# Copies of the late experts' outputs made on TensorE in place of DRAM, last writes split 48 and 16, and a new drawn order, in a two-layer MetaFormer kernel

## The chip, the core and the metric

The kernel runs as one program on one core of a Trainium2 chip. The core has five engines that run their own instruction streams in order: TensorE (PE, matrix products), VectorE (DVE), ScalarE (ACT), GpSimd (POOL) and SyncE (SP). SP, ACT and POOL also issue transfers between DRAM and the on-chip memory, which 16 DMA engines carry out. The metric is the device time of one execution in microseconds; lower is better. The time before is a median of 3786.38 us over three runs (3786.0 to 3797.89).

## What is computed

The input x has 32 images of 56 x 56 positions and 128 channels, all float32. Two layers run one after the other, each with a token mixer and a feed-forward part, both with a residual:

```python
# layer 0
x = x + conv_binary_3x3(batchnorm_sign(layernorm(x)))       # signs of weights and inputs
t = t + moe(layernorm(t))           # 8 experts of 128x128, the best 2 for each token
# layer 1
x = x + gate * (layernorm(triangle_product(a, b)) @ Wz + bz) # over each image's 56x56 grid
t = t + expert_choice(layernorm(t))
```

The change lies around the last step. Of an image's 3136 tokens, each of 64 experts chooses the 8 with the highest softmax probability (over the tokens):

```python
logits = einsum('bsd,ed->bse', x, gate_w); probs = softmax(logits, axis=1)
vals, idx = top_k(probs.transpose(0, 2, 1), 8)               # per image and expert: 8 tokens
pooled = einsum('bked,bke->bed', gathered, topv)             # the 8 tokens, summed by weight
h = gelu(pooled @ weight1 + bias1); out = h @ weight2 + bias2 # 64 experts, 128 -> 512 -> 128
outputs[b, idx] += topv * out        # ONE output row goes to eight tokens, with eight weights
```

So one output row of an expert for an image is written eight times, each time with another factor, added to eight different tokens. A token can be chosen by several experts.

## The kernel before

**Tiling.** The 32 images are worked as 16 pairs, p = 0 to 15. A pair's 6272 tokens are 7 units of 128 x 7 tokens, 128 channels each. A first pass over all 112 units gathers the batch statistics of layer 0 (until about 600 us). Then the pairs follow at a period of about 190 us, several of them overlapped: the convolution of one pair runs beside the mixture of experts, the triangle product and the last gates of earlier ones.

**The stages of a pair that matter here.** `moe_experts` (L812 on) loads, for each of 49 tiles of 128 tokens, the gates of 8 experts, repeated over all partitions, into a tile gb (SP, L821), multiplies it by the transposed tokens xT (VectorE, L827), and PE sums eight matmuls into acc (L832). xT is copied out of the transposes trm by ACT (L583). Before that the routing runs through PE's ps_rl and ps_r, a chain of small VectorE operations, and the transpose trg (L797) of the gates. `tri_turn` makes the transposes trt; `gate_turn` stores the pair's result to `out`; `top8` finds the 8 tokens of each expert and gathers them (POOL, L1222); `pool_rows` sums them and ends in the transpose tr_p.

**The late experts.** The 64 experts' weights (32 MB) are streamed twice. `late_experts(False, g)`, 16 groups g of four experts, serves the 26 images of pairs 0 to 12 and runs between the stages of pairs 13 to 15. `late_experts(True, g)` serves the last three pairs (LAST) at the end. Both load the weights (L1412, L1414), form ph (L1479), the transposes trh, the gelu on ACT, po (L1525), and add the bias on VectorE (L1533) into `side2.ap[:, 5, :]`, 128 rows: 4 experts x 32 images.

For pairs 0 to 12 the images form two lots of 14 and 12 (LOTS). Before, the group's rows are written to DRAM (`o_d`, L1541), then read back for each lot and expert with each row repeated eight times (L1551), into a tile `eo` with 112 or 96 rows for four experts. `eo` shares the buffers tagged xT. VectorE multiplies it by the gains (L1558), and POOL adds each expert's rows to the tokens in `out` by an indirect transfer (L1575), in which a lot's next addition waits for the last one's landing:

```python
for j in range(NE):
    nc.sync.dma_start(
        eo.ap[:rows, j, :],
        o_d[g][j, i0:i1, :].unsqueeze(1).to_broadcast([i1 - i0, K1, C]),
    )
```

A one-element memset, `between` (L1316), stands between POOL operations of different lots.

**The last three pairs.** `last_sums(p)` reads the chosen tokens of each of these pairs (POOL, L1666, 8 times 128 rows) into rows_last and builds a matrix m that says which experts' outputs belong to which row, so that each row is written once with all its additions. `last_load(half)` reads the outputs of 32 experts back from `o_last_d` into at_last (SP, L1689); `last_out_rows(p, half)` multiplies m by them (PE, L1708), adds them to the rows (VectorE, L1720) and writes four times 128 rows (POOL, L1731), so 12 writes for each half of the experts.

**What sets the order.** Each operation is recorded by `op(engine, ns, r=, w=, land=)` with what it reads and writes, a cost, and for transfers a time `land`. The stages get a rank from the table TICK. `Order.run` then plays the program through by these costs, picks for each engine the ready operation of lowest rank, subject to a fixed number of buffers for each tag (gb 5, xT 4, ps 8 PSUM banks, x 15, u 6), and emits the instructions in the order so found. The order of each engine is thus fixed when the program is built; on the chip each engine runs its own list and waits where something is late. SP's list holds all loads and most stores, so a transfer that waits for its buffer holds all that stand behind it.

Of the kernel before, what the change touches and what calls it, by code (L numbers as in the profile page):

```python
# [12 lines left out]
F32 = mybir.dt.float32  # L13
# [14 lines left out]
C = 128  # L28
N7 = 7
# [9 lines left out]
    "fetch": (1.58, 3.45, 5.52, -1.97, 9.89, 8.41, 11.94),  # L39
    "sign": (-0.24, 0.69, 0.62, 6.29, 6.36, 10.44, 7.52),  # L40
    "conv": (1.26, 2.47, 6.82, 8.46, 10.49, 11.27, 13.74),
    "conv_back": (3.04, 3.74, 6.89, 9.11, 10.54, 11.48, 14.87),
    "moe_turn": (4.55, 4.08, 9.93, 10.17, 12.05, 12.07, 15.21),
    "moe_gates": (7.93, 6.46, 10.3, 10.32, 15.22, 13.8, 15.72),
    "moe_experts": (10.11, 8.23, 10.44, 10.38, 15.35, 13.82, 17.26),
    "moe_add0": (14.4, 13.58, 10.89, 13, 17.91, 16.49, 17.47),
    "moe_add1": (12.35, 12.05, 11.31, 12.55, 16.09, 14.74, 18.98),
    "tri_turn": (16.03, 16.94, 19.18, 18.34, 19.2, 18.97, 19.62),
    "moe_stats": (4.06, 9.6, 11.95, 15.11),
    "moe_route": (6.11, 10.25, 12.5, 15.67),  # L50
    "tri_stats": (14.43, 14.07, 18.68, 19.34),
    "tri_b": (20.52, 21.37),
    "tri_a": (22.17, 21.41),
    "tri_z": (22.19,),
    "tri_out": (23.45, 23.11, 25.14, 25.06, 25.81, 28.13, 29.03),
    "gate_stats": (23.81, 25.31, 26.89, 30.24),
    "gate_turn": (25.22, 25.8, 26.84, 28.27, 29.66, 32.16, 31.08),
    "gate_logits": (26.8, 27.15, 28.55, 30.19, 30.4, 34.44, 34.71, 34.72),
    "clear": (32.94,),
    "top8": (36.55,),  # L60
    "pool_rows": (39.18,),
    "late_first": (27.19, 27.47, 30.26, 33.5, 37.45, 38.24, 40.16, 41.35, 43.38, 44.86, 45.85,
        48.06, 49.55, 51.3, 58.28, 60.22),
    "late_alone": (47.43, 50.82, 50.84, 53.47, 61.88, 67.39, 57.81, 65.6, 63.21, 71.67, 75.8,
        82.21, 97.17, 84.67, 68.82, 79.34),
    "last_sums": (70.63, 74.49, 77.96),
    "last_load": (68.66, 101.21),
    "last_rows": (91.82, 76.74, 99.71, 103.42, 119.45, 116.33),
# [4 lines left out]
NX, NY = 15, 6  # L73
# [212 lines left out]
def kernel(ctx: ExitStack, tc: tile.TileContext, a: dict, out: bass.AP):  # L286
# [12 lines left out]
    HB = B // 2  # L299
# [23 lines left out]
    make_identity(nc, ident)  # L323

# [42 lines left out]
    NL = 3  # L367
    LAST = range(NP - NL, NP)
    HB = 2 * ((NP - NL + 1) // 2)
    LOTS = ((0, HB), (HB, B - 2 * NL)) + tuple((2 * p, 2 * p + 2) for p in LAST)  # L370
# [3 lines left out]
    EH = E1 // 2  # L374
# [4 lines left out]
    o_d = [dram.tile([NE, B, C], F32, name=f"o_{g}") for g in range(E1 // NE)]  # L379
# [25 lines left out]
    with ExitStack() as c2:  # L405
# [21 lines left out]
        for t in lines:  # L427
# [3 lines left out]
            "x": NX, "u": NY, "ps": 8, "gb": 5, "xT": 4, "yl": 3,  # L431
            "st": 3, "q": 3, "lg": 1, "k1": 1, "k2": 1, "mk": 2, "d": 2,
            "gg": 2, "gT": 2, "rm": 4, "zq": 1, "lgT": 1,
            "m8": 2, "i8": 2, "sq": 2, "pg": 4, "near": 2, "pacc": 1, "ptc": NL + 1,
# [155 lines left out]
        def fetch(p, u):  # L590
            g = p * NU + u
            x_ = live[p]["x", u] = new("x", [128, N7, C], f"x_{NUT + g}")

            @op("SP", 360, w=parts(x_), land=1200)
            def _():
                nc.sync.dma_start(x_.ap, x_units[g])

        def sign(p, u):
# [3 lines left out]
            @op("SP", 360, r=[("y1_d", g)], w=[y], land=1200)  # L602
            def _():
                nc.sync.dma_start(y.ap, y1_d[g])
# [205 lines left out]
        def moe_experts(p, u, n):  # L810
# [8 lines left out]
            @op("SP", 360, r=[("gd", p, u)], w=[gb], land=1300)  # L819
# [136 lines left out]
        def tri_z(p):  # L956
# [71 lines left out]
            @op("SP", 360, r=[(zT, 0), (zT, 4)], w=[("z_d", p)], land=300)  # L1028
# [12 lines left out]
            for rg in range(4):  # L1041
                @op("SP", 720, r=[("z_d", p), zv], w=[(zv, rg)], land=300)
# [86 lines left out]
        def gate_turn(p, u):  # L1129
# [6 lines left out]
            @op(*issue, r=parts(x_), w=[("out", p, u)], land=1200)  # L1136
# [7 lines left out]
            @op(*issue, r=parts(y), w=[("y3", p, u)], land=1200)  # L1144
# [1009 lines left out]
```

## Time and profile before

| What | us |
|---|---|
| median of three runs | 3786.38 |
| the three runs | 3786.0, 3786.38, 3797.89 |
| the profiled execution, its own time | 3805.24 |
| its span, first to last instruction | 3803.4 |
| PE busy with matmuls in the span | 3427.8 |
| VectorE busy | 3191.5 |
| ScalarE busy | 2350.5 |
| POOL busy | 443.8 |
| mean granted clock of TensorE | 0.96 |

A profile line names an engine (PE, PEld for its weight loads, DVE, ACT, POOL, SP), a line of the code, an operation, and the tiles it writes and reads, with buffer numbers left out. "x128" is a count. After the bar stand the busy time in us, the mean of one in ns, and the idle time of the engine just before these instructions with what ended most of it. An engine's q (SPq) is its queue of transfers. In the list of waits a line says which instruction waited for which, for how many us in total, how often, and the longest. The chain of waits is followed back from the last instruction: at each step to what released it, or to the instruction before it on its engine. The rows of stages give, for a stretch of time, the busy time and count of each engine, the granted clock of TensorE (1.00 is full), the busy share of the DMA engines and GB/s. The profiled execution took 18.9 us more than the median of the runs.

### The profile page before, as it was taken

The numbers are of one execution on the slowest core, as the hardware profiler recorded it, in microseconds if no ns is written. First come the engines' busy times: TensorE is split into PE (matmuls) and PEld (weight loads), VectorE is DVE, ScalarE is ACT, GpSimd is POOL, SyncE is SP. The second block draws the span as 40 slices with busy tenths as digits, with TensorE's granted clock in tenths as the row PEclk, the third lists the DMA queues.
The fourth block names the chain that finished last, engine by engine and source line by source line (L and its number), as shares of the span: only waits on it lengthen the run. The fifth ranks groups of instructions, "written<-read, shape, count | busy, mean of one in ns | idle before, by whom it ended". The sixth has DMA issues, their size and how long they took to land.

```text
span 3803.4 us, 79485 instructions
## 1 busy us (share of the span) xinstructions
PE 3427.8 (90%) x28051; PEld 2791.8 (73%) x28051; DVE 3191.5 (84%) x10626; ACT 2350.5 (62%) x5438; POOL 443.8 (12%) x506
## 2 busy tenths in 40 slices
PE   7998999999999999999999999999999997876644
PEld 7886878787877777777777777777777775664422
DVE  7997979898989898989898989898989886765551
ACT  6997357575757666666666666666666664453420
POOL 0000000101010101010101010101010104234454
PEclk9999999999999999999999999999999998898667
DMA  7996747474747474747474747474747477687685
GB/s 292 358 356 226 256 155 268 151 272 148 276 150 268 146 268 153 269 154 269 154 269 156 265 155 268 157 267 158 265 160 262 163 251 210 201 248 227 184 238 163
DMA packets 358127, 842.03 MB, mean 221 GB/s; under 512 B 89169, under 2 KB 133154, under 8 KB 357730
## 3 DMA queue, kind: packets, MB, share of 16 engines
q1 hardware_dynamic: 298658, 719.02, 54.8%
q10 hardware_dynamic: 38080, 99.57, 6.6%
q0 software_dynamic: 20992, 18.37, 2.9%
q8 instruction: 223, 3.65, 0.4%
q14 instruction: 174, 1.43, 0.1%
HBM read 661.53 MB, written 175.23 MB: 220 GB/s over the span
## 4 chain that ended last, share of the span: by engine, by line
PE 44%; DVE 27%; DMA 14%; ACT 8%; issue 3%; SPq 2%; POOL 1%; another core or an unknown queue 0%; ACTq 0%; POOLq 0%; DVEq 0%
PE acc L832 21%; DMA gb<-gate 7%; DVE gb L827 5%; DVE stln L488 5%; PE gram L1799 4%; PE ps_cv L633 4%; PE tr L477 3%; PE ps_g L1067 2%; ACT yt L562 2%; DVE frame L611 2%; DVE x L575 2%; DMA w_True<-in_L_ffn_weight 2%; PE ps_z L976 2%; DVE x L1111 1%; DVE sg L1102 1%
## 5 line engine op out<-in xcount | busy, mean ns | idle before, releaser
L832 PE MATMUL acc<-expert_w,gb 128*128 128x128 f32 x12544 | 1473.6, 278 | 73.0 <-DVE gb L827 49.2
L832 PEld LDWEIGHTS acc<-expert_w,gb 128*128 128x128 f32 x12544 | 1437.7, 193 | 121.7 <-DVE gb L827 51.4
L827 DVE TENSOR_TENSOR gb<-gb,xT 128x1024 f32<-128x1024 f32 x784 | 949.3, 1220 | 95.3 <-DMA gb<-gate 91.3
L488 DVE BATCH_NORM_STATS2 stln<-x 128x6 f32<-128x128 f32 x2352 | 600.1, 287 | 1.9
L562 ACT ACTIVATE yt<-x,rmln 128x128 f32<-128x128 f32 x784 | 327.2, 495 | 203.6 <-DVE rmln L550 190.0
L562 ACT ACTIVATE yl<-x,rmln 128x128 f32<-128x128 f32 x756 | 324.2, 494 | 175.7 <-DVE rmln L547 125.3
L633 PE MATMUL ps_cv<-frame,w_sign 128*128 128x448 bf16 x2016 | 420.0, 357 | 8.3 <-DVE frame L611 8.3
L562 ACT ACTIVATE ym<-x,rmln 128x128 f32<-128x128 f32 x784 | 324.6, 486 | 66.9 <-DVE rmln L550 57.3
L633 PEld LDWEIGHTS <-w_sign 128*128 128x128 bf16 x2016 | 196.5, 98 | 174.4 <-DVE frame L611 8.5
L1222 POOL DMA_INDIRECT rows<-y,near x128 | 133.2, 1041 | 995.5 <-DVE k L738 795.7
L1575 POOL DMA_INDIRECT out<-eo_False,picked x128 | 198.1, 1548 | 317.1 <-DMA out<-eo_False,picked 137.0
L1118 POOL MEMSET a_bd<- 128x2048 f32 x15 | 27.1, 1807 | 1655.4 <-PE ps_zo L1089 1655.4
L562 ACT ACTIVATE y<-x,rm 128x128 f32<-128x128 f32 x448 | 210.5, 716 | 14.5 <-DVE rm L547 14.5
L1067 PE MATMUL ps_g<-wg,yT 128*128 128x128 f32 x1568 | 211.2, 283 | 0.0
L1067 PEld LDWEIGHTS ps_g<-wg,yT 128*128 128x128 f32 x1568 | 192.0, 195 | 20.5 <-issue 12.0
L583 ACT COPY xT<-trm 128x512 f32<-128x512 f32 x224 | 110.1, 529 | 151.6 <-PE trm L477 132.7
L641 ACT ACTIVATE cv<-ps_cv,cv_shift,cv_scale 128x448 f32<-128x448 f32 x224 | 159.2, 726 | 70.7 <-PE ps_cv L633 36.1
L844 DVE TENSOR_TENSOR x<-acc,x 128x512 f32<-128x512 f32 (+1 forms) x224 | 139.7, 623 | 73.7 <-PE acc L832 62.8
L1799 PE MATMUL gram<-y 128*128 128x128 f32 x1568 | 198.4, 279 | 0.0
L1799 PEld LDWEIGHTS gram<-y 128*128 128x128 f32 x1568 | 194.4, 200 | 0.5 <-issue 0.5
L488 DVE BATCH_NORM_STATS2 st<-x 128x6 f32<-128x128 f32 x784 | 179.6, 282 | 4.6 <-DMA x<-in_x 4.6
L583 ACT COPY ylT<-trl 128x512 f32<-128x512 f32 x224 | 113.7, 533 | 111.4 <-PE trl L477 102.0
(263 smaller groups left out, 5439.5 us busy)
## 6 DMA issues: line engine op xcount, KB each, us to landing
gb<-gate SPq DMA_DIRECT2D x784, 512.0 KB
x<-in_x SPq DMA_DIRECT2D x224, 448.0 KB
y<-yT SPq DMA_DIRECT2D x112, 448.0 KB
ys<-y SPq DMA_DIRECT2D x112, 448.0 KB
out<-x ACTq DMA_DIRECT2D x105, 448.0 KB
y<-yl ACTq DMA_DIRECT2D x105, 448.0 KB
w_False<-in_L_ffn_weight SPq DMA_DIRECT2D x128, 256.0 KB
w_True<-in_L_ffn_weight SPq DMA_DIRECT2D x102, 256.0 KB
```

What stands on the lines that cost most here:

```text
L488: nc.vector.bn_stats(st.ap[:, c0 + k, :], src.ap[:, k, :])
L562: nc.scalar.activation(dst.ap[:, k, :], src.ap[:, k, :], AF.Identity, bias=m, scale=r)
L583: nc.scalar.copy(t.ap[:, n0 : n0 + k, :].rearrange("c n p -> c (n p)"), ps.ap[:, : k * 128],)
L633: nc.tensor.matmul(acc, lhsT=w_sign[:, tap, :], rhs=frames[f][:, 8 * band + kh : 8 * band + kh + 8, kw : kw + W], start=(tap == 0), stop=( ...
L641: nc.scalar.activation(cv.ap[:, :, 64 * h : 64 * h + 64], ps.ap[:, :448].rearrange("c (q n) -> c n q", n=N7), AF.Identity, bias=cv_shift, ...
L827: nc.vector.tensor_tensor(gb.ap, gb.ap, over(xT.ap[:, n, :], E0), ALU.mult)
L832: nc.tensor.matmul(acc.ap[:, n % 4 * C : (n % 4 + 1) * C], lhsT=gb.ap[:, e, :], rhs=expert_w[:, e * C : (e + 1) * C], start=(e == 0), stop ...
L844: nc.vector.tensor_tensor(dst, acc.ap[:, : k * C], dst, ALU.add)
L1067: nc.tensor.matmul(psg.ap[:, n * C : (n + 1) * C], lhsT=yT[:, n0 + n, 16 * u : 16 * u + 16, :].rearrange("c r v -> c (r v)"), rhs=wg, star ...
L1222: nc.gpsimd.indirect_dma_start(out=rows.ap[:, j, :], out_offset=None, in_=y3_d[p], in_offset=bass.IndirectOffsetOnAxis(ap=near.ap[:, k + j ...
L1575: ins = nc.gpsimd.indirect_dma_start(out=tokens_out, out_offset=bass.IndirectOffsetOnAxis(ap=picked[lot][:rows, e : e + 1], axis=0), in_=e ...
L1799: nc.tensor.matmul(gram.ap[:, :C], lhsT=y.ap[:, n, :], rhs=y.ap[:, n, :], start=(g % G16 == 0 and n == 0), stop=(g % G16 == G16 - 1 and n ...
```

## The change

Three things are changed together.

First, the eight copies. A constant `spread` holds, for each of the four 32-row blocks and each lot, ones such that a matmul with it repeats each image's row eight times. PE makes, for each of a group's four experts, both lots' copies in one PSUM bank `ps_eo`, straight from the group's rows; VectorE multiplies them out of PSUM by the gains, one instruction for each expert and lot, into a tile `eo` of its own tag with four buffers, each for one expert and both lots. `o_d` and its writes and reads are gone. POOL adds the two lots of an expert one after the other. The buffers tagged xT become three.

Second, the last writes. In place of two halves of 32 experts, `PARTS` splits them into 48 and 16: three writes of 128 rows for each image of a pair in the first part, one in the second, so 18 and 6 writes in all.

Third, the order. The costs `land` of most transfers are set anew (a gate load 1392 for 1300 ns, a weight load 868 for 700, the pooled store 5600 for 1500, and others), so is POOL's cost of a last write (1000 for 1500), and every entry of TICK is new. This moves instructions on all engines and in all stages. Some lines are added to serve four last pairs; with NL = 3 they do nothing.

```diff
 TICK = {
-    "fetch": (1.58, 3.45, 5.52, -1.97, 9.89, 8.41, 11.94),
+    "fetch": (-2.04, 1.47, 6.43, -9.37, 9.91, 4.03, 12.95),
...
-    "last_load": (68.66, 101.21),
-    "last_rows": (91.82, 76.74, 99.71, 103.42, 119.45, 116.33),
+    "last_load": (79.71, 120.93),
+    "last_rows": (102.26, 131.4, 121.75, 140.19, 135, 143.81),
 }
...
-NX, NY = 15, 6
+NX, NY, NEO = 15, 6, 4
...
+    spread = const.tile([128, 2, HB * K1], F32, name="spread")
+    for q in range(0, 128, B):
+        for k, (i0, i1) in enumerate(LOTS[:2]):
+            nc.vector.tensor_copy(
+                spread[q : q + B, k, : (i1 - i0) * K1].rearrange("b (i k) -> b i k", k=K1),
+                along(ident[q : q + B, q + i0 : q + i1], K1),
+            )
...
-    EH = E1 // 2
+    PARTS = ((0, 1, 2), (3,))
...
-            "x": NX, "u": NY, "ps": 8, "gb": 5, "xT": 4, "yl": 3,
+            "x": NX, "u": NY, "ps": 8, "gb": 5, "xT": 3, "yl": 3, "eo": NEO,
...
-            @op("SP", 360, r=[("gd", p, u)], w=[gb], land=1300)
+            @op("SP", 360, r=[("gd", p, u)], w=[gb], land=1392)
...
-                @op("SP", 720, r=[("o_d", g)], w=[eo], land=300)
-                def _(eo=eo, i0=i0, i1=i1, rows=rows):
-                    for j in range(NE):
-                        nc.sync.dma_start(
-                            eo.ap[:rows, j, :],
-                            o_d[g][j, i0:i1, :].unsqueeze(1).to_broadcast([i1 - i0, K1, C]),
-                        )
...
-                @op("DVE", 600, r=[("picked", p) for p in range(i0 // 2, i1 // 2)], w=[eo])
-                def _(eo=eo, lot=lot, rows=rows):
-                    nc.vector.tensor_tensor(
-                        eo.ap[:rows, :NE, :], eo.ap[:rows, :NE, :],
-                        along(gains[lot][:rows, es], C), ALU.mult,
-                    )
...
+            for j in () if alone else range(NE):
+                ps_e = bank(f"ps_eo_{name}_{j}")
+
+                @op("PE", 2 * 222, r=[(side2, "o")], w=[ps_e])
+                def _(q=B * j, ps_e=ps_e):
+                    for k, (i0, i1) in enumerate(LOTS[:2]):
+                        rows = (i1 - i0) * K1
+                        nc.tensor.matmul(
+                            ps_e.ap[:rows, k * C : (k + 1) * C],
+                            lhsT=spread[q : q + B, k, :rows], rhs=side2.ap[q : q + B, 5, :],
+                            start=True, stop=True,
                         )
...
+                eo = new("eo", [128, 2, C], f"eo_{name}_{j}")
...
+                    def _(eo=eo, lot=lot, rows=rows, e=e, ps_e=ps_e, k=lot):
+                        nc.vector.tensor_scalar(
+                            eo.ap[:rows, lot, :], ps_e.ap[:rows, k * C : (k + 1) * C],
+                            gains[lot][:rows, e : e + 1], None, ALU.mult,
+                        )
...
-            for half in range(2):
-                put(NP - 1, "last_rows", 3 * half + i, last_out_rows, p, half)
-        for half in range(2):
-            put(NP - 1, "last_load", half, last_load, half)
+            for k in range(len(PARTS)):
+                put(NP - 1, "last_rows", NL * k + i, last_out_rows, p, k)
+        for k in range(len(PARTS)):
+            put(NP - 1, "last_load", k, last_load, k)
```

## The prediction

> **What bounds the kernel now.** I read the stages first, then the chain of waits of the late stage, then its waits and instruction groups, and last the order in which the two kernels' instructions stand on each engine.
>
> ```profile
> core 0: us, PE busy (x) PEld busy (x) DVE busy (x) ACT busy (x) POOL busy (x), PEclk, DMA share, GB/s
> 600.00:2800.00 2200.00, 2114.00 (x17380) 1732.76 (x17381) 2009.56 (x6333) 1454.34 (x3266) 133.37 (x114) 1.00 0.60 211
> ...
> 3100.00:3640.00 540.00, 393.67 (x3109) 297.61 (x3105) 329.10 (x1024) 273.00 (x548) 200.40 (x224) 0.83 0.75 224
> 3640.00:3772.00 132.00, 68.92 (x697) 36.41 (x697) 52.47 (x161) 20.44 (x34) 67.83 (x94) 0.75 0.75 208
> 3772.00:3803.40 31.40, 4.51 (x56) 3.98 (x56) 2.65 (x7) 0.23 (x1) 15.41 (x29) 0.54 0.12 39
> ```
>
> Until 3100 us the kernel is bound by TensorE: 2114 of 2200 us busy at full clock. From 3100 to 3640, where the late experts run between the last three pairs, PE is busy for 394 of 540 us at a clock of 0.83; 146 us are waits. From 3640 to 3772 the last weights stream in, and from 3772 the last rows are written. What the 540 us wait for, by the chain of waits of that stretch and by its waits:
>
> ```profile
> by line: DMA gb<-gate 10.6%; issue 8.5%; DMA out<-eo_False,picked 6.4%; DMA w_False<-in_L_ffn_weight 6.0%; PE acc L832 5.9%; POOL out L1575 4.8%; SPq L1551 4.5%; DMA eo_False<-o 3.5%; DMA w_False<-pooled_d 3.4%; PE ps_g L1067 3.1%; PE ps_cv
> ```
>
> ```profile
> SPq L1551 <- DMA out<-eo_False,picked: 51.3, 7, 9.7
> ```
>
> ```profile
> POOL out L1575 <- DMA out<-eo_False,picked: 131.7, 43, 9.4
> ...
> DVE eo_False L1558 <- DMA eo_False<-o: 46.0, 15, 13.1
> ```
>
> ```profile
> L1558 DVE TENSOR_TENSOR eo_False<-eo_False,gains 112x512 f32<-112x512 f32 x16 | 11.1, 691 | 30.0 <-DMA eo_False<-o 29.5 <-issue 0.4
> ...
> L1242 DVE SCALAR_TENSOR_TENSOR acc<-rows,pg,acc 128x128 f32<-128x128 f32 x112 | 39.0, 348 | 10.3 <-DMA rows<-y,near 7.3 <-issue 1.0 <-DVE acc L1242 1.0
> ```
>
> The round trip of the late outputs through DRAM is on the path: SP issuing copies 4.5% (24.3 us), their landing 3.5% (18.9), together 43 us, and the row adds with their landings another 11.2% (60 us). SP was held 51 us at L1551 for a buffer that the row adds had not yet released, with weights and gate loads queued behind it; VectorE stood 46 us for the copies.
>
> **The change, part by part.** [...]I work out a difference and take it from the median.
>
> *Copies.* Gone: 16 writes to o_d (L1541), 128 copy issues on SP (L1551, median 781 ns, about 100 us of SP in all) with 6.8 MB in rows of 512 bytes, and 32 multiplies (L1558, 22.1 us). In the new order no such copy is left on SP (1967 SP instructions become 1823), so the change does what it says. Added: 128 matmuls and 128 multiplies from PSUM.
>
> The nearest row for the matmul is ps_zo (L1089), 17 rows deep, 128 columns: 87.2 us for 1568 records, 55.6 ns each, two records per float32 matmul. 128 x 2 x 55.6 ns = 14 us at full clock, 17 at 0.83. Against it speaks the Trainium skill, "TensorE: Matmul & The Clock Gate", Part 1: the array runs at half clock until about 3.4 us of sustained work, and a matmul of 128 columns then takes 106.7 ns. These matmuls lie in a stage full of gaps, so by the page 27 us. I take 17, because the row of the stages grants 0.83 here; 27 is the far end. PE has 146 us of waits in the stage, and 394/540 of its time is taken, so I charge 0.73 x 17 = 12 us.
>
> The multiply reads PSUM. The nearest rows are L1533 (128x128 from PSUM, 287 ns) and L1242 above (348). "VectorE: DVE Perf Modes", section "Why PSUM operands drop a tier", says that a float32 scalar multiply from SBUF could run at double rate and one from PSUM cannot. So no discount: 128 x 0.29 = 37 us, 15 more than the 22 removed; at double rate it would be about 7 more. VectorE had 211 us idle in the stage, 46 of them waiting for these copies, so I charge 0; uncovered it is 15.
>
> On the path, then: 43 us of copy issue and landing go, 12 come. The row adds stay: 128, each behind the landing of the last one to the same half. Over the 34 adds whose wait ended by such a landing, the median from one to the next of a half is 7.1 us. POOL now alternates halves strictly; its `between` memsets go from 141 to 161, 20 x 0.44 = 9 us on an engine 37% busy: 0. What is late next is the gate loads (10.6%, 57 us) and weight loads (6.0%), which share the DMA engines with the 6.8 MB, about 6% of the stage's 121 MB: some 4 us less. 43 - 12 + 4 = **35 us gained**. From both sides: if all 146 us of waits fell to the 4% of the main stage, 100; if the adds' chain is held elsewhere, a loss (second rival).
>
> *The new order in the main stage.* The clearest difference of the orders is in the gate loads. A gb buffer is free when the matmuls of five tiles earlier end; from there SP issues, the load lands (5.4 to 8 us in the chain of waits), VectorE multiplies (1.22 us), and PE goes on: 7 to 10 us. I summed the PE work, by the rows' time per matmul, that stands between these two points, over pairs 5 to 10 (294 tiles): before, 102 tiles had under 10 us and 30 under 8; now 24 and none. The waits this concerns, from 600 to 3000 us:
>
> ```profile
> PE acc L832 <- DVE gb L827: 19.9, 30, 1.3
> ```
>
> ```profile
> DVE gb L827 <- DMA gb<-gate: 52.8, 69, 3.1
> ```
>
> PE lost 19.9 us to it directly; "<- DVE q_ln L517" (13.3) in the same list stands before the same matmuls. Three quarters of these 33 us would be 25. Against it, other leads shrink: PE work from routing (ps_r) to the gates' transpose from at least 11.2 to 7.4 us, from trt to the first ps_b from 3.0 to 0.5; PE already waits 22 us at trg (L797). I give back 10: **15 us gained**, between -35 (all leads' waits, 89 us, cut by 40%) and +20 (the shrunk leads cost 1.5 us in each of 13 pairs). xT with 3 buffers in place of 4: from trm to the first matmul of its tile the least PE work is 28.3 us before, 29.6 now, so 0; if the cover fails, up to 10, ACT's wait for it in before being 9.6 us at L583.
>
> *At the start.* Eight small copies build the constant on VectorE, 8 x 0.17 = 1.4 us; VectorE waits for the first x until 4.17 us, so 0, else 1.4.
>
> *Last writes in 48 and 16 experts.* Before, 12 last writes stood behind the last weight, now 6:
>
> ```profile
> 3782.09 0.97 POOL L1731 DMA_INDIRECT out<-rows_last,at_last  x1 [6.85 <-DVE rows_last L1720]
> 3783.05 0.09 POOL L1316 MEMSET between<- 1x1 f32 x1
> 3783.36 0.97 POOL L1731 DMA_INDIRECT out<-rows_last,at_last  x1 [0.23 <-DVE rows_last L1720]
> ```
>
> At 1.27 us each that would save 7.6 us. But the new order puts the first part's matmuls behind ph_True of all of groups 14, 12 and 13 on PE, and its at_last load behind the very last weight on SP. So 18 + 6 writes follow the last landing, where 12 did (the first 12 ran from 3754.6 to 3775.2, beside the loads). From the last landing (3772): ph 2.4, po 1.1, six matmuls 1.7, an add 0.5, and slack 0.6 = 6.3; 24 x 1.27 = 30.5; to the end 6.3 (3797.1 to 3803.4): 43 us, against 31 now, 4.2 of those an unexplained stall. 12 us lost; if the last loads come early, less. I take **10 lost**, from 8 gained to 16 lost. Between 3640 and 3772 little changes: 79 big weight loads follow near_d of pair 15 in place of 77, at 1.44 us each 3 more; 12 copies go, about as much.
>
> Sum: -35 - 15 + 10 = -40: 3786 - 40 = **3746**.
>
> **Rivals.**
>
> *The whole round trip pays (0.12).* Copies and most adds leave the chain, since SP no longer stands 51 us before everything behind it: 103 us of chain minus 12 is 91, with -15 and +10: 3786 - 96 = 3690. For it: SP's blocked time is shared by all loads. Against: each add still waits for a landing.
>
> *The row adds hold VectorE (0.20, slower).* There are four eo tiles, one expert each, freed when both adds have landed. VectorE runs in order; a multiply that finds no free tile stops all of VectorE, and with it four of eight PSUM banks. The place is groups 10 to 12, after pair 14's top-8: 12 experts stand within 33 us of VectorE work, about 44 us of time at the stage's share. At s us an expert the adds need 12 s, four tiles cover 4 s, so the hold is 8 s - 44: 13 us at 7.1, 40 at 10.5 (groups 6 to 9 would add 12 s - 109 = 17, 13 to 15 8 s - 75 = 9). At 10.5, 66 in all: 3786 - 40 + 66 = 3812. It decides from about 9.5 us on, where the hold eats the 40. For it: spacings of 9.0 to 10.4 us stand around 3400. Against: the median is 7.1, and fewer bytes compete.
>
> *Nothing comes of it (0.12).* The next waits, gate and weight loads, land where the copies landed; closing +10, the order's gain -15: 3781.
>
> **The numbers.** A measurement of this kernel tells about 0.3% (11 us) from no change. Forecast 0.56, faster by over 0.3%; with the first rival 0.68. Same 0.12, slower 0.20. The forecast's own range is 3710 to 3775; it must reach to the first rival and near the second for 8 in 10: 3692 to 3806.
>
> **What would show it.** Right: no copies on SP; VectorE's 46 us at L1558 gone and no such wait on the eo multiply; the stretch from the first late add to pair 15's top-8 some 35 us shorter; gb waits on VectorE in 600 to 3000 well under 52.8; some 24 last writes in a row after the last weight. Wrong: "DVE eo <- DMA out" of tens of us (second rival), or a main stage whose period, now 190.4 us from top-8 to top-8, has not shortened.

## The result, and the profile after

Five runs of the changed kernel took 3763.8 to 3775.2 us, median 3770.89; the kernel before took 3786.0 to 3807.5 beside it, median 3797.89. The ratio is 0.9927, with a 95% interval from 0.9901 to 0.9954: faster by 0.5 to 1.0%. The forecast was 40 us less than before, and 27 were measured (the two profiled executions differ by 34). The sign and nearly the size are right, but the parts that make the sum are not those of the prediction.

The start of each pair's top-8 (the MAX8 on VectorE, one per pair of images) cuts the run into stretches. Starts are in us of each profiled execution, the pairs counted from 0; spans are 3803.4 before and 3769.1 after:

| | first top-8 | to pair 12's | period | pair 12 to 13 | pair 13 to 15 | pair 15 to end |
|---|---|---|---|---|---|---|
| before | 686.3 | 2293.1 | 191.1 | 202.9 | 442.3 | 178.7 |
| after | 689.6 | 2327.4 | 193.9 | 203.8 | 383.4 | 165.0 |
| difference | +3.2 | +34.3 | +2.9 | +0.9 | -58.9 | -13.7 |

So the main stage lost 37.5 us where 15 were to be gained, the late stage gained 59 where 35 were forecast, and the tail gained 14 where 10 were to be lost. The rows of the stages, with the tail cut where the last weights are in:

```profile
core 0: us, PE busy (x) PEld busy (x) DVE busy (x) ACT busy (x) POOL busy (x), PEclk, DMA share, GB/s
600.00:2800.00 2200.00, 2106.91 (x17156) 1732.89 (x17155) 1990.76 (x6257) 1440.10 (x3190) 130.40 (x111) 0.99 0.60 209
3100.00:3640.00 540.00, 437.78 (x3886) 339.01 (x3884) 401.95 (x1335) 304.90 (x616) 237.61 (x264) 0.89 0.79 239
3640.00:3720.00 80.00, 49.76 (x540) 23.63 (x543) 38.02 (x112) 14.52 (x25) 42.24 (x56) 0.77 0.96 290
3720.00:3769.10 49.10, 10.60 (x160) 8.40 (x152) 6.54 (x17) 1.74 (x3) 25.30 (x47) 0.60 0.12 40
```

In the main stage PE is as busy as before, 96%, but ran 17156 matmuls in the 2200 us and not 17380, and its clock is 0.99 in place of 1.00. From 3100 to 3640 PE is busy for 438 us and not 394, at 0.89 and not 0.83. From 3640 to 3720 the weights move at 290 GB/s (208 before, from 3640 to 3772). The chain of waits of the late stage:

```profile
by line: PE acc L838 16.0%; DMA out<-eo_False,picked 13.4%; issue 6.0%; DVE stln L494 4.9%; DVE gb L833 4.2%; DMA rows<-y,near 3.4%; DVE sg L1108 2.6%; PE ps_cv L639 2.6%; DMA w_False<-in_L_ffn_weight 2.4%; PE ps_g L1073 2.1%; DVE x L1117 2
```

The copies are gone from it, and the waits that were called "late next" are less: gate loads (10.6% before) are no longer among the first, and weight loads are 2.4% (6.0 before). Matmuls lead, and behind them the landings of the row adds. The waits of the same stretch:

```profile
POOL out L1588 <- DVE eo_False L1575: 119.6, 20, 42.2
...
POOL out L1588 <- DMA out<-eo_False,picked: 55.7, 22, 5.1
DVE eo_False L1575 <- DMA out<-eo_False,picked: 32.4, 12, 5.9
```

(Columns: us in all, times, longest.) GpSimd now stands mostly for the next product (119.6 us, 78.2 before) and less for the adds' landings (55.7, 131.7 before). VectorE's 46 us for copies are gone; 32 us for a free eo tile have come. What the new instructions cost, from the instruction groups of the whole run:

```profile
L1575 DVE TENSOR_SCALAR eo_False<-ps_eo_False,gains 112x128 f32<-112x128 f32 (+1 forms) x128 | 37.2, 341 | 39.2 <-DMA out<-eo_False,picked 32.4 <-issue 4.6 <-PE ps_eo_False L1557 2.0
...
L1557 PE MATMUL ps_eo_False<-w_False,spread 32*96 32x128 f32 (+1 forms) x256 | 14.6, 311 | 10.3 <-DVE w_False L1539 9.5 <-ACT lgT L1177 0.9
```

A multiply from PSUM has a mean of 341 ns (0.29 us was assumed), but the two of an expert overlap, and VectorE is busy with all 128 for 37.2 us, the 37 of the prediction. The 256 matmul records keep PE busy for 14.6 us: near the 14 that the prediction has for full clock, below its 17 and 27. And the waits of the main stage, 600 to 3000 us, with PE's wait at trg in the kernel before behind them:

```profile
PE acc L838 <- DVE gb L833: 36.9, 53, 2.0
...
PE trg L803 <- DVE stln L494: 22.8, 8, 2.9
DVE gb L833 <- DMA gb<-gate: 22.3, 36, 1.6
PE trg L803 <- DVE gg L789: 10.4, 14, 2.9
```

```profile
PE trg L797 <- DVE k L779: 14.4, 11, 1.4
```

VectorE waits 22 us for gate loads in place of 53, as the prediction had it from the leads. But PE's wait for gate products went up, from 19.9 to 36.9, and its waits at trg from 14.4 us, the longest 1.4, to 33 (22.8 and 10.4), the longest 2.9. What that wait does is seen in PE's timeline of one pair and in the stages of 4 us around it:

```profile
2067.25 0.93 PE L483 MATMUL trc<-ident,cv 128*128 128x128 f32 x7
2068.50 1.48 PE L483 MATMUL trt<-ident,yt 128*128 128x128 f32 x4 [0.32 <-ACT yt L568]
2072.83 0.63 PE L803 MATMUL trg<-ident,gg 128*56 128x128 f32 x2 [2.85 <-DVE stln L494]
2073.26 1.06 PE L483 MATMUL trc<-ident,cv 128*128 128x128 f32 x4
```

```profile
2066.00:2070.00 4.00, 3.49 (x19) 1.87 (x17) 3.89 (x15) 2.77 (x6) 3.23 (x4) 1.00 0.12 33
2070.00:2074.00 4.00, 1.17 (x6) 1.12 (x7) 4.00 (x16) 3.76 (x10) 2.28 (x2) 0.74 0.17 51
2074.00:2078.00 4.00, 4.00 (x24) 1.98 (x25) 3.33 (x15) 1.11 (x2) 0.00 (x0) 0.50 0.24 76
```

PE stands 2.85 us, and from then on the granted clock is 0.50: four transposes of trc take 1.06 us. It happens once in nearly every pair. Added up in slices of 2 us between 600 and 3020, the clock withheld (slice times one less the clock) is 32 us; in the kernel before it is 3.4.

### The profile page after: what moved, and what is told of

The parts are those of the page before. It is cut to its first block, busy times and chain, and to the rows that moved or that the text cites. A ratio compares the mean times of both kernels' runs of the same rounds, so it can differ in the third digit from the quotient of the medians.

```text
span 3769.1 us, 79927 instructions
## 1 busy us (share of the span) xinstructions
PE 3440.6 (91%) x28307; PEld 2811.6 (75%) x28307; DVE 3223.4 (86%) x10730; ACT 2371.0 (63%) x5436; POOL 464.6 (12%) x526
## 4 chain that ended last, share of the span: by engine, by line
PE 49%; DVE 34%; DMA 8%; issue 5%; ACT 3%; POOL 1%; another core or an unknown queue 0%; ACTq 0%; SPq 0%; POOLq 0%; DVEq 0%
PE acc L838 22%; DVE gb L833 8%; PE ps_cv L639 6%; DVE stln L494 5%; PE gram L1843 4%; DMA gb<-gate 4%; PE tr L483 3%; DMA out<-eo_False,picked 2%; DVE sg L1108 2%; DVE x L1117 2%; DVE x L581 2%; PE trc L483 2%; DVE frame L617 2%; PE ps_b L896 2%; PE ps_z L982 1%
## 5 line engine op out<-in xcount | busy, mean ns | idle before, releaser
L494 DVE BATCH_NORM_STATS2 stln<-x 128x6 f32<-128x128 f32 x2352 | 569.9, 288 | 2.5
L1083 ACT ACTIVATE sg<-ps_g 128x512 f32<-128x512 f32 x224 | 115.2, 537 | 224.7 <-PE ps_g L1073 219.8
L1588 POOL DMA_INDIRECT out<-eo_False,picked x128 | 216.7, 1693 | 235.7 <-DVE eo_False L1575 119.6
L1073 PE MATMUL ps_g<-wg,yT 128*128 128x128 f32 x1568 | 203.4, 279 | 8.6 <-DVE eo_False L1575 5.5
L581 DVE TENSOR_TENSOR x<-trc,x 128x512 f32<-128x512 f32 (+1 forms) x224 | 132.6, 619 | 81.5 <-PE trc L483 80.1
L494 DVE BATCH_NORM_STATS2 st<-x 128x6 f32<-128x128 f32 x784 | 187.5, 284 | 6.4 <-DMA x<-in_x 6.4
```

The source lines that it names most:

```text
L494: nc.vector.bn_stats(st.ap[:, c0 + k, :], src.ap[:, k, :])
L581: nc.vector.tensor_tensor(xf, ps.ap[:, : k * 128], xf, ALU.add)
L1073: nc.tensor.matmul(psg.ap[:, n * C : (n + 1) * C], lhsT=yT[:, n0 + n, 16 * u : 16 * u + 16, :].rearrange("c r v -> c (r v)"), rhs=wg, star ...
L1588: ins = nc.gpsimd.indirect_dma_start(out=tokens_out, out_offset=bass.IndirectOffsetOnAxis(ap=picked[lot][:rows, e : e + 1], axis=0), in_=e ...
```

## The experiments

Times are medians beside the kernel before on the same chip (3798 to 3801 us; 3785 for the last run), ratios with 95% intervals. "Withheld" is the clock sum just named. The stretches are those of one profiled execution each. e1 to e4 stand on one chip, e5 to e8 on a second, e9 and e10 on a third, e11 on a fourth:

| | ratio | first top-8 | period | 12 to 13 | 13 to 15 | 15 to end | withheld |
|---|---|---|---|---|---|---|---|
| changed | 0.9927 | 689.6 | 193.9 | 203.8 | 383.4 | 165.0 | 32 |
| e1_fill | 0.9865 | 688.9 | 192.0 | 204.7 | 389.7 | 163.3 | 3.3 |
| e2_behind | 0.9904 | 694.2 | 193.7 | 205.6 | 386.5 | 164.0 | 34 |
| e3_copies | 1.0133 | 715.5 | 194.6 | 234.8 | 394.6 | 173.5 | 26 |
| e4_order | 1.0439 | 677.5 | 201.4 | 204.2 | 453.8 | 207.2 | 68 |
| e5_xt3 | 1.0279 | 716.3 | 195.2 | 200.1 | 455.6 | 193.9 | 34 |
| e6_bias | 0.9880 | 690.0 | 191.8 | 203.2 | 383.9 | 166.9 | 1.7 |
| e7_halves | 0.9929 | 689.1 | 193.6 | 203.5 | 376.8 | 160.6 | 29 |
| e8_double | 0.9946 | 691.4 | 193.4 | 205.6 | 389.6 | 169.8 | 31 |
| e9_acts | 0.9906 | 691.4 | 191.7 | 203.2 | 380.7 | 171.6 | 1.7 |
| e10_fill4 | 0.9866 | 690.5 | 192.3 | 204.7 | 382.8 | 163.7 | 20 |
| e11_busy | 0.9870 | 690.4 | 191.7 | 202.7 | 384.3 | 149.5 | 1.7 |

**The gap ahead of trg and the clock.**

```diff
             @op("PE", 110, r=[gg], w=[trg])
             def _():
+                for _ in range(8 if u == batches[0][0] else 0):
+                    nc.tensor.matmul(trg.ap[:, 128:256], lhsT=ident, rhs=ident, start=True, stop=True)
```

> The changed kernel with eight matmuls of ident by ident (a result that nothing reads, in a free corner of the bank of trg) ahead of the first trg transpose of each pair of images; the order is else the same. In the trace of the changed kernel PE stands 2.85 us there in nearly every pair, and the granted clock then falls to 0.50 for some 5 us: 35 us of clock lost between 600 and 3120 us, 3.4 in the kernel before. Theory A (the gap trips the clock): the 2.0 us of filler lie inside the gap, the clock stays at 1.00, the time from top-8 to top-8 falls from 193.8 to about 191.4 us, and the run is some 30 us shorter than the changed kernel's 3771: 3741. Theory B (the longer period is made of late gate products and the clock is only a sign of it): the period stays at 193.8 or grows by the filler, 3771 to 3790.

Measured: 3752.7 us, ratio 0.9865 (0.9845 to 0.9885). The clock stays up:

```profile
2058.74 1.48 PE L485 MATMUL trt<-ident,yt 128*128 128x128 f32 x4 [0.30 <-ACT yt L570]
2060.06 1.95 PE L806 MATMUL trg<-ident 128*128 128x128 f32 x16
2063.07 0.40 PE L809 MATMUL trg<-ident,gg 128*56 128x128 f32 x2 [1.06 <-DVE k L787]
2063.31 0.60 PE L485 MATMUL trc<-ident,cv 128*128 128x128 f32 x4
```

The gates come no earlier (trg still starts 3.0 us after trt ended), but the transposes behind it take 0.60 and not 1.06 us. Pair 12's top-8 starts at 2993.1 and not 3017.0: 23.9 us for work that computes nothing. Theory A holds. The gain is less than the 29 us of clock returned: PE now waits 1.0 us in each pair at tr_a for ScalarE's lines, which the slow clock had hidden (10.1 us in ten pairs, 1.0 in the changed kernel).

With half the filler (the 8 becomes 4):

> The filler ahead of trg with four matmuls in place of eight (1.0 us of the 2.85 us gap). Theory A of the main stage (the clock falls when PE does too little in a stretch of some 3 us, however the idle time lies in it; with the work moved ahead of trg in an earlier run the gap was split into four of 0.3 to 1.4 us and the clock still fell): 1.9 us stay idle there and the clock falls in part of the pairs: a loss between 3 and 37 us of clock between 600 and 3120 us, the period between 192.0 and 193.9. If the longest single gap decides, and 1.4 us of idle in one piece are harmless as in the kernel before, 1.9 in one piece falls at least sometimes: the same range; with a loss under 5 us in both it is the total that counts.

Measured: 3749.1 us, ratio 0.9866 (0.9849 to 0.9883). The clock still falls in ten of twelve pairs, for a shorter time; 20 us are withheld, and the period is 192.3. Most of the gain is there with a good part of the clock still lost, so microseconds of clock and of run are not one to one. It cannot tell one long gap from the total.

The other way to fill the gap was to let work that is there anyway go first:

```diff
 op.run(), once the order is drawn up, for pairs 2 to 12
-PE: trt x4, trg(0), trg(1), trc x4, trt x3, trc x3, ps_b ...
+PE: trt x4, trc x4, trt x3, trc x3, trg(0), trg(1), ps_b ...
```

> The changed kernel with one move: in pairs 2 to 12 the two trg transposes of units 0 and 1 stand behind the next three transpose groups on PE (2.8 us of work) in place of ahead of them; nothing else moves on any engine. Theory A (the stall ahead of trg and the clock that it trips): both go, PE's wait at trg falls from 28 to under 8 us in ten pairs, the clock is 1.00, the period falls from 193.8 to about 190.9 us in eleven pairs: 32 us shorter than 3771, 3739. Theory B (late gate products): the gates come 2.8 us later, VectorE's gate products wait more, and the period stays: 3771 or above.

Measured: 3765.9 us, ratio 0.9904 (0.9888 to 0.9920); the period is 193.7. PE's timeline of a pair shows why:

```profile
2074.20 1.48 PE L502 MATMUL trt<-ident,yt 128*128 128x128 f32 x4 [0.30 <-ACT yt L587]
2075.96 0.66 PE L502 MATMUL trc<-ident,cv 128*128 128x128 f32 x4 [0.28 <-ACT cv L666]
2077.98 0.47 PE L502 MATMUL trt<-ident,yt 128*128 128x128 f32 x1 [1.36 <-ACT yt L587]
2078.84 0.86 PE L502 MATMUL trt<-ident,yt 128*128 128x128 f32 x2 [0.39 <-ACT yt L587]
```

The stall at trg is gone, and the work moved ahead stands for ScalarE instead, which was late too: four gaps of 0.3 to 1.4 us, 2.3 in all. The clock falls as before (34 us withheld): no single gap has to be long. My expectation failed at the cover: I took the three groups as ready because they had run without a wait, but they had run behind the stall.

**The parts of the change by themselves.** In e3_copies the changed kernel is given back the ticks, landing costs and halves of before (GpSimd's cost of a last write stays as changed):

```diff
-TICK, land=..., PARTS = ((0, 1, 2), (3,))   # of the changed kernel
+TICK, land=..., PARTS = ((0, 1), (2, 3))    # of the kernel before
```

> The copies by TensorE alone: the changed kernel with the ticks, the landing costs and the halves of the last writes of the kernel before, its order drawn up from those. Theory A (the copies carry the gain, the new order loses in the main stage): period about 191 us, the stretch from pair 13's top-8 to pair 15's top-8 near 385 us (442 before, 383 changed), and about 60 us less than the kernel before: 3738, faster than the changed kernel. Theory B (the new order carries the gain of the late stage): that stretch stays above 430, and the time within 15 us of the kernel before. My prediction's own term for this part was 35 us.

Measured: 3854.2 us, ratio 1.0133 (1.0114 to 1.0153): slower than before. Half of theory A stands: the late stretch is 394.6 us under the old ticks too. The other half fell: the first top-8 comes 29 us later than before, the period is 194.6, and the stretch from pair 12 to 13 is 32 us longer. The reverse, the kernel before with the new ticks and landing costs:

> The new order alone: the kernel before, copies through DRAM kept, with the ticks and landing costs of the changed kernel, its order drawn up from those. Theory A (the order loses in the main stage and the copies carry the gain): if the gap ahead of trg comes with the ticks, the period is 193 to 194 us, the late stretch stays near 440, and the run is 20 to 40 us longer than the kernel before: 3820 to 3835. Theory B (the order carries the gain of the late stage): the stretch from pair 13's to pair 15's top-8 falls to 385 to 400 also here, and the run is near the changed kernel's 3771.

Measured: 3968.0 us, ratio 1.0439 (1.0423 to 1.0455). The late stretch stays at 453.8 us, so the order does not carry the late gain. The main stage is far worse than expected, with a period of 201.4. Ticks and resources belong together: each set slows the other's kernel. Which resource it is was tested in the kernel before by one number:

```diff
-            "x": NX, "u": NY, "ps": 8, "gb": 5, "xT": 4, "yl": 3,
+            "x": NX, "u": NY, "ps": 8, "gb": 5, "xT": 3, "yl": 3,
```

> The kernel before with one number changed: three xT buffers in place of four (ticks, landing costs, DRAM copies and halves as before; the order is drawn up from them). The run with the copies by TensorE alone had 715 us at the first top-8 (686 before) and a period of 194.6 us (191.1 before) although no late expert runs there; the one thing that differs there besides a constant is this buffer. Theory A (the third xT buffer less costs the main stage under the old ticks): first top-8 near 715, period near 194.5, and with the DRAM copies sharing three buffers the run is 60 us or more longer than the kernel before, above 3860. Theory B (my prediction's zero for xT was right and the copies' other resources did it): period near 191, first top-8 near 686.

Measured: 3904.5 us, ratio 1.0279 (1.0245 to 1.0313), with the first top-8 at 716.3 and the period at 195.2: those of e3_copies. Theory A holds. The fourth xT buffer, in whose place the eo tiles stand, is worth 105 us of span under the old ticks (3803.4 to 3908.7). The mean period hides where the main stage loses: the first four periods of e5_xt3 are 200 to 209 us, the next eight 190 to 192, as before. With the old ticks the buffer's price is paid at the start, 30 us ahead of the first top-8 and 50 in the four pairs behind it, while the changed kernel's periods are 192 to 196 us from first to last. Between e5_xt3 and e3_copies the ticks, the halves and the xT buffers are the same: 455.6 becomes 394.6 us from pair 13 to 15, 193.9 becomes 173.5 behind it, 200.1 becomes 234.8 ahead of it, and the span falls by 55.7 us. That is what the copies bring by themselves, with three xT buffers and the old ticks.

TensorE's side of the copies, by doing each matmul twice:

```diff
-                    for k, (i0, i1) in enumerate(LOTS[:2]):
+                    for k, (i0, i1) in 2 * list(enumerate(LOTS[:2])):
```

> The changed kernel with each of the 256 matmuls by the constant of ones made twice, the second into the same place with the same values: it prices TensorE's side of the copies by itself. My prediction charged 12 us of path for the first set (17 us at the clock of the stage, times the share of PE's time that is taken). Theory A: 12 us longer, 3783. Theory B (PE waits for row adds, landings and VectorE in that stage): within 4 us of the changed kernel. Above 17 us: PE is the bound of the stage and the second rival is wrong in its place.

Measured: 3776.8 us, ratio 0.9946 (0.9929 to 0.9963), against 0.9927 (0.9901 to 0.9954): 0.2%, some 7 us, inside the intervals. It speaks against PE as the bound of the stage, and cannot tell 4 us from 12.

**The tail.** In the changed kernel the first part's 18 writes and the second part's 6 do not follow in a row. GpSimd, then VectorE:

```profile
3745.89 0.97 POOL L1775 DMA_INDIRECT out<-rows_last,at_last  x1 [0.23 <-issue]
3746.85 0.09 POOL L1322 MEMSET between<- 1x1 f32 x1
3755.43 0.97 POOL L1775 DMA_INDIRECT out<-rows_last,at_last  x1 [8.50 <-DVE rows_last L1758]
```

```profile
3732.73 0.29 DVE L1539 TENSOR_TENSOR w_True<-po_True,w_True 128x128 f32<-128x128 f32 x1 [6.52 <-remote]
3734.23 0.69 DVE L1517 TENSOR_TENSOR hs_True<-trh_True,b 128x512 f32<-128x512 f32 x1 [1.21 <-remote]
3749.81 0.29 DVE L1539 TENSOR_TENSOR w_True<-po_True,w_True 128x128 f32<-128x128 f32 x1 [14.89 <-remote]
```

The gap of 8.5 us puts the 19th write 8.3 us later than the usual 1.27 us from write to write would. The adds of the last two groups stand 6.5 and 14.9 us for "remote", a releaser that this view does not name. The second goes on 3.9 us after the start of the 18th write. Their matmuls end, by the profile, at 3725.9 and 3737.6. One suspect was the bias that these adds read, loaded last of all. On top of e1_fill, with only this moved (in words):

```diff
 SP, late_alone, groups 12 and 13
-... last weight; at_last loads; bias(12); bias(13)
+... last weight of the group; bias of the group; ...; at_last loads
```

> The kernel with the filler ahead of trg, and on SP the loads of the second bias of the last two groups (12 and 13) moved ahead, directly behind those groups' last weight; nothing else moves. In the tail VectorE's adds of these two groups stood 6.5 and 14.9 us for something that the trace does not name, while GpSimd wrote the first 18 rows; the second add is what the last six writes wait for, and GpSimd stood 8.3 us between its 18th and 19th write. Theory A (the landing of these late bias loads is held up): the two stalls go, the gap between the 18th and the 19th write falls to under 1 us, and the run is 8 us shorter than with the filler alone: 3745. Theory B (VectorE itself is held while GpSimd issues its writes): the stalls stay where they are, the gap stays at 8.3 us, 3752.

Measured: 3751.7 us, ratio 0.9880 (0.9855 to 0.9905). The stalls are 5.1 and 14.9 us, the gap is 8.5: the bias is not it. Next the halves of before in the changed kernel (PARTS = ((0, 1), (2, 3))):

> The changed kernel with the last writes in two halves of 32 experts again (12 writes and 12), all else as changed. The counting of the prediction: six more writes at 1.27 us stand behind the last load, 7.6 us longer, 3778. Theory B of the tail (VectorE's last add is held until GpSimd has issued the first part's writes): the first part is 12 writes, not 18, so GpSimd is done 7.6 us earlier, the last add and everything behind it come 7.6 us earlier, and the end is where it was: 3771. Theory A of the tail (a bias load lands late for another reason): 3778.

Measured: 3768.9 us, ratio 0.9929 (0.9902 to 0.9956): the same time with twelve writes behind the gap as with six. The hold is shorter with the first part's writes, 9.3 us and not 14.9:

```profile
3726.50 0.29 DVE L1539 TENSOR_TENSOR w_True<-po_True,w_True 128x128 f32<-128x128 f32 x1 [9.34 <-remote]
```

It is released 3.2 us after the start of the 12th write (3723.31), as before after the 18th. So what the 48/16 split saves behind the gap it adds ahead of it. To see whether VectorE is what is held, both adds of the two groups were taken off it, on top of e1_fill (in words):

```diff
-VectorE: hs = trh + b1, ScalarE: hG = gelu(hs);  VectorE: o = po + bias
+ScalarE: hG = gelu(trh, bias=b1) in 16 pieces;   TensorE: po += ident x bias, ScalarE: o = po
```

> The kernel with the filler ahead of trg, and the last two late groups (12 and 13) taken off VectorE: the first bias enters as the bias of 16 Gelu instructions on ScalarE that read the bank of trh, the second bias is added on TensorE by four matmuls with the identity, and ScalarE copies the sum out. Nothing else moves. Theory B (VectorE's instructions are held while GpSimd issues its row writes; other engines are not): the outputs of group 13 are written out some 10 us after the first part's writes begin, not 28 us after, and the gap between GpSimd's 18th and 19th write falls from 8.3 us to at most 4 (to 0.3 if the six row adds of VectorE that follow get through, to 3 or 4 if they are held until the 18th write is done): 4 to 8 us less than the filler alone. Theory A (every wait for a semaphore or a landing is held in that time, whatever the engine): the gap stays at 8 us.

Measured: 3762.1 us, ratio 0.9906 (0.9886 to 0.9925); the gap is 12.6 us. ScalarE now stands:

```profile
3720.14 0.27 ACT L1568 COPY w_True<-po_True 128x128 f32<-128x128 f32 x1 [20.37 <-remote]
3723.71 2.96 ACT L1541 ACTIVATE hG_True<-trh_True,b 128x32 f32<-128x32 f32 x16 [3.31 <-remote]
```

Theory B fell: it is not VectorE. And theory A, "every wait", does not hold either: TensorE and SP went on at once in that time. What the held instructions have in common is that they read a bank that TensorE filled just before it fell idle. So TensorE was given work, on top of e1_fill (in words):

```diff
 PE, group 13
-... trh; po (waits for hG); ps_last (waits for at_last)
+... trh; 14 x (ident by ident); po; 20 x (ident by ident); ps_last
```

> The kernel with the filler ahead of trg, and TensorE kept busy in the tail: 14 matmuls of ident by ident (3.5 us at full clock, nothing reads them) ahead of the last group's second matmuls (po of group 13) and 20 (5 us) behind them; nothing else moves. In all runs so far the instructions that stood in the tail while GpSimd wrote rows were readers of a bank that TensorE had just filled, on VectorE and, when the work was moved there, on ScalarE (20.4 us); ScalarE reading what VectorE had written, and TensorE waiting for ScalarE, went on at once; and TensorE had nothing to do after the bank in question. Theory C (the last matmuls before TensorE falls idle are reported done late, the recorded end being modelled): with work behind them the adds of groups 12 and 13 follow their matmuls within 1 us, the gap between GpSimd's 18th and 19th write falls from 8.3 us to under 2, and the run is 6 to 8 us shorter than with the filler alone: 3744. Theory D (what holds them comes from GpSimd's row writes, whatever TensorE does): stalls of 6 and 15 us and a gap of 8 us as before, 3751.

Measured: 3731.9 us beside 3784.5, ratio 0.9870 (0.9849 to 0.9892). VectorE's timeline, with GpSimd's 18th and 19th write behind it:

```profile
3692.04 0.28 DVE L1549 TENSOR_TENSOR w_True<-po_True,w_True 128x128 f32<-128x128 f32 x1
3692.60 0.69 DVE L1523 TENSOR_TENSOR hs_True<-trh_True,b 128x512 f32<-128x512 f32 x1 [0.29 <-issue]
3696.72 0.29 DVE L1549 TENSOR_TENSOR w_True<-po_True,w_True 128x128 f32<-128x128 f32 x1 [3.42 <-PE po_True L1541]
```

```profile
3711.74 0.97 POOL L1789 DMA_INDIRECT out<-rows_last,at_last  x1 [0.23 <-issue]
3713.01 0.97 POOL L1789 DMA_INDIRECT out<-rows_last,at_last  x1 [0.22 <-issue]
```

In this run nothing is held, and 24 writes follow in a row, 1.27 us apart. But that TensorE's new work did it is not shown. This run alone stands on the fourth chip, where the kernel before takes 3784.5 us and not 3798 to 3801, and the holds are gone from all of it, also where its instructions are those of e1_fill. The bias add of one late group of pairs 0 to 12, some 95 us ahead of the first of the new matmuls, in e1_fill and then in e11_busy:

```profile
3611.12 0.29 DVE L1545 TENSOR_TENSOR w_False<-po_False,w_False 128x128 f32<-128x128 f32 x1 [3.88 <-remote]
```

```profile
3596.09 0.28 DVE L1549 TENSOR_TENSOR w_False<-po_False,w_False 128x128 f32<-128x128 f32 x1
```

In e1_fill's list of waits "remote" ends 49 us of waiting by VectorE and ScalarE, in e11_busy's none.

What "remote" is can be read from the trace in another place: it keeps the times at which TensorE counts up the semaphore that its readers wait for. In the changed kernel the counts for the three held instructions come at 3732.70, 3734.15 and 3749.79 us. That is 6.8, 7.6 and 12.2 us after the profile's (modelled) ends of their matmuls, and 0.02 to 0.08 us before the readers start. So the readers waited for TensorE, whose matmuls were done, or reported done, late: this half of theory C is shown, and it clears the bias loads and VectorE as well. In each of the twelve profiles other than e11_busy, 16 to 33 of TensorE's counts, some 5200 to 5630 in each, come over 1 us after the last matmul end that the profile draws, every one of them beside an indirect transfer of GpSimd. In e11_busy none comes more than 0.15 us late, though TensorE stands idle for over 2 us beside such a transfer 21 times. Whether work behind a bank keeps its count from coming late stays untested, because the new work and the chip changed together.

The ratio does not tell this kernel from e1_fill either (0.9870 and 0.9865; 8 us are 0.2%, and the intervals are twice that), and the 149.5 us from pair 15's top-8 to the end, 163.3 in e1_fill, are no measure of the new work. Both kernels are faster than the changed kernel by some 0.6%.

## Why the prediction was right in sum and wrong in its parts

That the sum came out near is luck. In spans, the main stage up to pair 13's top-8 missed its forecast by 53 us to the bad, the late stage and the tail missed theirs by 24 us each to the good, and these nearly cancel.

*The copies, 35 gained.* The mechanism was right and the size too small. By themselves the copies gain 56 us (e5_xt3 to e3_copies), and from pair 13's to pair 15's top-8 even 61. The first late add to pair 15's top-8 was to be 35 us shorter: it is 423 and not 498 us, 75 shorter, 16 of them because the first add comes that much later after pair 12's top-8. The 43 us of copy issue and landing did go. The term that was mis-sized is the "some 4 us" for what was late next: SP's blocked time held weight and gate loads too. Gate loads fell out of the first places of the chain, and after the start of pair 15's top-8 the last weights were issued within 115 us and not 143, where the prediction said that little changes. How much each of these brought is not shown. The 12 us charged for TensorE fit the double run's 7, whose error is some 12. The 15 us of dearer multiplies came as 15 (37.2 us against 22.1); that they lay beside other work was not tried by itself.

*The main-stage order, 15 gained.* This step failed: 34 us were lost to the period and 3 at the start. The leads of gb were read rightly, as far as they go: VectorE's wait for loads fell by 30 us. The failed term is "I give back 10" for the leads that shrink. The one from ps_r to trg was named, from 11.2 to 7.4 us, and the far end of the range had the right idle time, 1.5 us in each of 13 pairs. (The 22 us that the prediction reads as PE's wait at trg are those of its weight loads; the matmuls' own wait was 14.4.) But idle time was all that was charged. The gap of 2.85 us lowered the clock for the work behind it: filling it returned 24 of the 37.5 us. Of the 13.6 that are left, PE's wait for gate products is a part (26.8 us in e1_fill, 19.9 before); the rest is open. A warning was at hand: the prediction weighs the Trainium skill, "TensorE: Matmul & The Clock Gate", Part 1, for the copies, and not for the lead. The same page, under "Why this matters for your kernels", advises against idle gaps above some 3 us between bursts of matmuls; here 2.85 us in one piece, or 2.3 in four, did it.

*xT, 0.* PE's cover was compared between two orders that had each been drawn up for their own buffers. So it did not show that the third order, the old ticks with three buffers, is 105 us slower. The new ticks are not a gain beside the copies: they buy back most of what the copies' tiles take from xT. Changed one after the other in this sequence, the sum in spans is +105 for the buffer, -56 for the copies, and -84 for ticks, landing costs and writes: -34 with rounding.

*The start, 0.* The first top-8 comes 3.2 us later.

*The last writes, 10 lost.* The tail from pair 15's top-8 is 13.7 us shorter, because the last weights were issued earlier. From there to the end the counting was right in kind: 49 us pass from the last group's ph (3720) to the end, where 43 were predicted and 31 were before. But the writes are not in a row. The stall called unexplained (4.2 us before) is 21 us in all, and it makes the split worth nothing: e7_halves has the same time. It is TensorE's late count in the kernel before too, at 3776.36 us for matmuls that end, by the profile, at 3773.36.

*The rivals.* The row adds do hold VectorE through the four eo tiles, for 32 us, two thirds of it between 3395 and 3460 us, ahead of pair 14's top-8 where the prediction put it behind. Where an add waited for a landing, the spacing of one lot was 6.8 us (7.1 before), well below the 9.5 from which this rival decides. "The whole round trip pays" was nearer the late stage and the tail (73 us) than the forecast.

## What to carry to other kernels

Charge a stall of TensorE for more than its length: look at the granted clock in the slices behind it, and ask whether a couple of us of idle work ahead of the wait costs less than the slow clock. When a change takes a buffer from a pool and redraws an order, price the buffer with the old order held fixed; otherwise its price hides in the order. When an instruction waits for something that a view does not name, look for the semaphore's own counts in the trace before moving work about. And before a cure is believed, look whether the trouble is gone also where the cure is not: in e11_busy it was.

## What the runs showed that was not expected

Readers of TensorE's last banks stood 5 to 20 us in the tail while GpSimd wrote rows, on VectorE and on ScalarE, because TensorE's counts came late. In the changed kernel, e1_fill, e6_bias and e7_halves the last of them went on 3.2 to 4.0 us after the start of the last write of the first part. That GpSimd's writes set the length is suggested by e7_halves; how they hold up TensorE's count, or its matmuls, stays open, and so does why the run on the fourth chip shows nothing of it. An unnamed stall elsewhere is the same thing: for the 8.8 us at 3201.8 in the kernel before, TensorE's counts start at 3210.62, 8.7 us after the last matmul end that the profile draws.

The granted clock fell to 0.50 after 2.85 us of idle time within 5 us, and also after 2.3 us spread over four gaps; with 1.06 us left behind 2.0 us of filler it did not.
